# Layer norm 1 of a fused convolution-attention network: who issues the value weights, and where the turned tiles stand

## The chip, the core and the metric

The kernel runs on one core of a Trainium2 chip. The metric is the device time in microseconds (us); of several runs the median is given. Everything is in 32-bit floats.

The core's engines are TensorE (PE, with its weight loads as PEld), VectorE (DVE), ScalarE (ACT) and GpSimd (POOL). SyncE (SP) issues DMAs. Each engine works through its own instructions in order. DMAs are issued on SP's queue (q1 in the profile) or on GpSimd's (q0), and both feed the same 16 DMA engines.

## What is computed

The input is a feature map of 4 x 16 x 16 positions with 1024 channels, taken as 1024 tokens. Three layers follow one another, each added to its input:

```python
x = x + L0_conv(_gn(x))                    # group norm, then a position-dependent mixing ("lambda") layer
t = _to_tokens(x)                          # (4, 256, 1024)
t = t + L1_attn(_ln_t(t))                  # layer norm 1, causal attention with 16 heads
t = t + L1_ffn(_ln_t(t))                   # layer norm 2, eight experts behind a gate

def _ln_t(v, eps=1e-5):
    m = jnp.mean(v, axis=-1, keepdims=True)
    s = jnp.var(v, axis=-1, keepdims=True)
    return (v - m) / jnp.sqrt(s + eps)
# in L1_attn:
qkv = jnp.einsum('btc,oc->bto', x, W_attn) + b_attn     # q, k and v of every token
```

The change lies where the first layer's output becomes the attention's input: layer norm 1, and the first products for v.

## The kernel before

The 1024 tokens are eight tiles of 128 rows. A tile's rows lie on partitions, as the norm needs them; TensorE wants channels on partitions, so every normalised tile has to be transposed into `ln1`.

**One pass of the loop (lines 622 to 641).** `spread(i)` is the last part of the first layer. For the tile after the present one, `content` (L452) makes two products per bank, which VectorE adds to `s0` (L460). Then 16 products (L603) give the present tile's output, which VectorE adds to `xs[t]` (L610). `layer_norm` takes mean and variance on VectorE (L197, L199, `inverse_root` L141 to L143, L169), and ScalarE writes the normalised rows to one of three slices of the tile `ln_rows` (L170). GpSimd then adds the attention's output bias to `xs[t]` (L638) and stores it to DRAM as `x_rows` (L639). Tiles are taken in the order 1, 3, 5, 7, 0, 2, 4, 6 of the token tiles; "tile i" below is the i-th in that order.

**Two ways to transpose.** For tiles 0 to 5, `turn_by_rows` stores the normalised rows to DRAM on SP (L212), waits for that to land, and reads them back with four DMAs (`quarters_of`, L182), so that the 32-row groups stand where they belong. `turn_quarters` then transposes 32 x 32 blocks on VectorE (L187). The quarters' buffers are spare space: the tile `emb` for even tiles and `s_w` for odd ones among tiles 0 to 3, and two buffers of their own for tiles 4 and 5. The turn of tile i - 2 stands behind the norm of tile i. Tiles 6 and 7 are transposed on TensorE (L219) and copied out by ScalarE (L223).

**The order.** From line 621 to line 755 a manual schedule holds: every engine executes in the order in which the code issues. The value weights come as two halves of 2 MB each, `w_v0` and `w_v1`, loaded by `w_tile` (L129). `w_v0` is issued on SP in the fourth pass (i = 3), behind that tile's quarters. `w_v1` is issued on SP after the loop, and takes the memory of `ln_rows`.

**Behind the loop (lines 718 to 733).** GpSimd makes sums of blocks of `w_v0` (`sums_v`, L160 to L163), since v is computed by a scheme of seven block products instead of eight. `first(0, t)` makes products 1 and 2 for token tile t (two groups of eight, L665); ScalarE copies the first one's bank (L683) and `second` adds the other one on VectorE (L688). Token tiles 1 and 3 (tiles 0 and 1 of the loop) come first. Then follow the norm of tile 7, the transposes of tile 6, the turn of tile 5, the products for token tile 0, the transposes of tile 7, and the products for token tile 2. After that VectorE sums blocks of `ln1` (`sums_of_B`, L695 to L699) for the remaining products.

PSUM banks come from rings of three, `mm` and `tr`; a product waits until the bank's last reader is done.

Of the kernel before, what the change touches and what calls it, by code (L numbers as in the profile page):

```python
# [32 lines left out]
F32 = mybir.dt.float32  # L33
# [6 lines left out]
P = 128  # L40
C = 1024
# [4 lines left out]
NT = TOK // P  # L46
# [3 lines left out]
REL = 2 * SIDE - 1  # L50
# [7 lines left out]
HALF = 512  # L58
# [4 lines left out]
Q = 4  # L63
# [6 lines left out]
def kernel(  # L70
# [27 lines left out]
    nc = tc.nc  # L98

    def pool(stack, name, bufs=1, **kw):  # L100
        return stack.enter_context(tc.tile_pool(name=name, bufs=bufs, reuse_waits="tile", **kw))
# [21 lines left out]
    def w_tile(name, *parts, home=None, queue=nc.sync):  # L123

        w = (home or wpool).tile([P, NC, HALF], F32, tag="w", name=name)
        at = 0
        for part in parts:
            n = part.shape[1]
            queue.dma_start(w[:, :, at : at + n], part.rearrange("(c p) n -> p c n", p=P))  # L129
            at += n  # L130
        return w
# [7 lines left out]
    def inverse_root(dst, var, eps):  # L139

        nc.vector.tensor_scalar(dst, var, eps, None, ALU.add)  # L141
        nc.scalar.activation(dst, dst, AF.Sqrt)
        nc.vector.reciprocal(dst, dst)  # L143
# [23 lines left out]
    def normalised(row, of, mean, rstd):  # L167
        less = small.tile([P, 1], F32, tag="ln_less", name="ln_less")
        done = nc.vector.scalar_tensor_tensor(less, mean, -1.0, rstd, ALU.mult, ALU.mult)  # L169
        nc.scalar.activation(  # L170
            row.rearrange("p (f c i) -> p c f i", f=Q, c=NC),
            of.rearrange("p (c f i) -> p c f i", c=NC, f=Q),
            AF.Identity,
            bias=less,
            scale=rstd,
        )
        return done
# [7 lines left out]
    def turn(row_T, row, slots=P):  # L185

        nc.vector.transpose(  # L187
            row_T[:, :, :slots].rearrange("p c (g j) -> p g c j", j=32),
            row[:, : slots // 32, :].rearrange("p g (c i) -> p g c i", c=NC),
        )  # L190

    def layer_norm(ln, t, on_pe=False):


        stats = small.tile([P, 2, 6], F32, tag="ln_stats", name=f"ln1_stats{t}")
        for j in range(2):
            nc.vector.bn_stats(stats[:, j, :], xs[t][:, ts(j, HALF)])  # L197
        mv = small.tile([P, 2], F32, tag="ln_mv", name=f"ln1_mv{t}")
        nc.vector.bn_aggr(mv, stats)  # L199
        rstd = small.tile([P, 1], F32, tag="ln_rstd", name=f"ln1_rstd{t}")  # L200
        inverse_root(rstd, mv[:, 1:2], EPS)
        if on_pe:
            less = small.tile([P, 1], F32, tag="ln_less", name=f"ln1_less{t}")
            nc.vector.scalar_tensor_tensor(less, mv[:, 0:1], -1.0, rstd, ALU.mult, ALU.mult)
            for j in range(2):
                nc.scalar.activation(ln[:, ts(j, HALF)], xs[t][:, ts(j, HALF)], AF.Identity, bias=less, scale=rstd)
            return
        normalised(ln, xs[t], mv[:, 0:1], rstd)

    def turn_by_rows(ln, t, quarters, turns):  # L210
        rows = turns.tile([P, Q, C // Q], F32, tag="rows", name=f"ln1_rows{t}")
        nc.sync.dma_start(rows.rearrange("n f c -> n (f c)"), ln)  # L212
        quarters_of(rows, quarters)
# [7 lines left out]
    def turned_on_pe(dst, t, banks):  # L221
        for j, pt in enumerate(banks):
            nc.scalar.copy(dst[:, 4 * j : 4 * j + 4, ts(t, P)], pt.rearrange("p (c n) -> p c n", c=4))  # L223
# [3 lines left out]
    with ExitStack() as layer0:  # L227
        l0 = pool(layer0, "l0")
# [7 lines left out]
        vp = l0.tile([P, 4, 2], F32, tag="vp", name="vp")  # L236
        for i, a in enumerate((v_gamma, v_beta, v_mean, v_var)):
            nc.gpsimd.dma_start(vp[:, i, :], a)
        emb = l0.tile([P, 2, REL, REL], F32, tag="emb", name="emb")
        v_T = l0.tile([P, 2, TOK], F32, tag="v_T", name="v_T")  # L240

        q0 = l0.tile([P, 2, SIDE, SIDE, BH], F32, tag="q0", name="q0")
# [1 line left out]
        with ExitStack() as projection:  # L244
# [96 lines left out]
            with tc.manual_schedule():  # L341
# [6 lines left out]
                for c in range(NC):  # L348
# [10 lines left out]
                    elif NC - 4 < c < NC - 1:  # L359
                        n = c - (NC - 3)  # L360
# [15 lines left out]
            for pair in range(2):  # L376
                a = [xn[:, 4 * j : 4 * j + 4, ts(4 + 2 * pair + i, P)] for i in range(2) for j in range(2)]
# [9 lines left out]
            for n in (1, 2, 3, 5, 4, 7, 6):  # L387
                for pair, ((a11, a12, a21, a22), (c11, c12, c21, c22), (s1, s2, s3, s4)) in enumerate(pairs):
                    a, b = {
                        1: (a11, b11),  # L390
                        2: (a12, b21),
                        3: (s4, b22),
                        5: (s1, b11),
                        4: (a22, b21),
                        7: (s3, b12),
                        6: (s2, b22),
                    }[n]
# [133 lines left out]
        s_w = tpool.tile([P, 3, NC // 2, P], F32, tag="s_w", name="s_w", bufs=1)  # L531
# [46 lines left out]
        for b, nt in tiles:  # L578
            t = 2 * b + nt
# [6 lines left out]
        ln_rows = wpool.tile([P, 4, C], F32, tag="w", name="ln_rows")  # L586
# [4 lines left out]
        def spread(i):  # L591
            b, nt = tiles[i]
            t = 2 * b + nt
            if i == 0:
                content(b, nt)
            if i + 1 < NT:
                content(*tiles[i + 1])
            for hp in range(2):
                py = mm(f"py{t}_{hp}")
                for hl in range(2):  # L600
                    bh = b * HEADS0 + 2 * hp + hl
                    for mh in range(2):
                        nc.tensor.matmul(  # L603
                            py[:, ts(hl, M)],
                            s0[:, mh, ts(nt, S2), :, bh].rearrange("p i j -> p (i j)"),
                            v_T[:, mh, ts(b, M)],
                            start=(mh == 0),
                            stop=(mh == 1),
                        )
                nc.vector.tensor_add(xs[t][:, ts(hp, HALF)], xs[t][:, ts(hp, HALF)], py)  # L610
            return t

        def turn_quarters(i):
            of, quarters = to_turn[i]
            turn(ln1[:, :, ts(of, P)], quarters)

        spare = [
            of[:, :C].rearrange("p (f c) -> p f c", f=Q)
            for of in (emb.rearrange("p c i j -> p (c i j)"), s_w.rearrange("p a c n -> p (a c n)"))
        ]  # L620
        in_order.enter_context(tc.manual_schedule())
        for i in range(NT - 1):
            t = spread(i)
            quarters = None
            if i < NT - 2:
                if i < NT - 4:
                    quarters = spare[i % 2]
                else:
                    quarters = late.tile([P, Q, C // Q], F32, tag="xg", name=f"ln1_quarters{t}")
            to_turn.append((t, quarters))  # L630
            layer_norm(ln_rows[:, i % 3, :], t, i >= NT - 2)
            if i >= 2:
                turn_quarters(i - 2)
            if i < NT - 2:
                turn_by_rows(ln_rows[:, i % 3, :], t, quarters, turns)
                if i == 3:
                    w_v = [w_tile("w_v0", W_attnT[:, 2 * C : 2 * C + HALF])]
                nc.gpsimd.tensor_add(xs[t], xs[t], bp)  # L638
                nc.gpsimd.dma_start(x_rows[ts(t, P), :], xs[t])  # L639
            else:  # L640
                nc.sync.dma_start(x_rows[ts(t, P), :], xs[t])
        t = spread(NT - 1)
# [4 lines left out]
    with ExitStack() as attention:  # L647
# [31 lines left out]
        def homes(r, t):  # L679
            return [v1[2 * r + i][:, 4 * l + t, :] for i in range(2) for l in range(2)]  # L680

        def first(r, t, *tags):
            nc.scalar.copy(homes(r, t)[3], one(r, t, 1, *tags[:1]))  # L683
            return r, t, one(r, t, 2, *tags[1:])

        def second(r, t, bank):
            c11, c12, c21, c22 = homes(r, t)
            nc.vector.tensor_add(c11, bank, c22)  # L688
# [23 lines left out]
        def sums_v(r, engine):  # L712
            a11, a12, a21, a22 = blocks_v(r)
            s1, s2, s4 = (s_v[:, r, i, :, :] for i in range(3))
            sums_of_A(a11, a12, a21, a22, s1, s2, s4, engine)


        sums_v(0, nc.gpsimd)
        seconds = [first(0, 1, tr, tr), first(0, 3, mm, tr)]
        layer_norm(ln_rows[:, (NT - 1) % 3, :], t, True)  # L720
        two = ps.tile([P, 2, HALF], F32, tag="sc", name="ln_two", bufs=1)
        banks = two[:, 0, :], two[:, 1, :]
        turn_on_pe(ln_rows[:, (NT - 2) % 3, :], banks)
        turned_on_pe(ln1, to_turn[NT - 2][0], banks)
        turn_quarters(NT - 3)
        for done in seconds:
            second(*done)
        second(*first(0, 0, mm, mm))
        banks = tr("ln_pt0"), mm("ln_pt1")
        turn_on_pe(ln_rows[:, (NT - 1) % 3, :], banks)  # L730
        turned_on_pe(ln1, t, banks)
        second(*first(0, 2, tr, tr))
        x_home.close()
        sums = ExitStack()
# [196 lines left out]
        queue = [(pair, n) for pair in range(1, NPAIR - 2) for n in (1, 2, 6, 7, 4, 5, 3)]  # L931
# [166 lines left out]
    with ExitStack() as gating:  # L1098
# [6 lines left out]
        quarters = l2.tile([P, E], F32, tag="quarters", name="quarters")  # L1105
# [665 lines left out]
```

## Time and profile before

| what | us |
|---|---|
| median of 3 runs | 1221.26 (1220.8 to 1224.78) |
| the profiled execution: its own time | 1225.42 |
| the profiled execution: its span | 1223.6 |
| TensorE busy in the span | 1208.8 |
| VectorE busy | 719.4 |
| GpSimd busy | 404.7 |
| ScalarE busy | 203.9 |
| mean granted clock of TensorE, as a share of full speed | 0.998 |

Times in the timelines are counted from the start of the span; layer norm 1 lies between about 218 and 285 us. "Idle before" is the time an engine stood still ahead of an instruction, with the instruction or DMA that ended the wait. A granted clock of 1.00 is full speed.

### The profile page before, as it was taken

Reading aid. Unit: us, or ns where it says so; the run is one execution under the profiler, and the core shown is the slowest. Engines: PE = TensorE matmul, PEld = TensorE weight load, DVE = VectorE, ACT = ScalarE, POOL = GpSimd, SP = SyncE. Lnnn points to the kernel's source line nnn. Section 1 sums busy time; section 2 is a strip of 40 time slices with the busy share of each in tenths; the row PEclk is TensorE's granted clock in tenths of the full one; section 3 lists DMA queues with packets and bytes.
Section 4 is the critical chain, followed back from the end, with each engine's and each line's share of the span. In section 5 each row is a group of like instructions: output and inputs, shape, how many; then the busy total and the mean of one; then the engine's idle time right before and its main releaser. Section 6 shows DMA issues by size and latency. Waiting matters only on the chain.

```text
span 1223.6 us, 13265 instructions
## 1 busy us (share of the span) xinstructions
PE 1208.8 (99%) x4780; PEld 632.7 (52%) x4780; DVE 719.4 (59%) x1256; ACT 203.9 (17%) x505; POOL 404.7 (33%) x467
## 2 busy tenths in 40 slices
PE   9999999999999999999999999999999999999998
PEld 5444884777884444454544444444344334434443
DVE  5796636567423665566654657576565656565732
ACT  3310111111000222222221212101111111111110
POOL 1051341264000222222232117427453635463521
PEclk9999999999999999999999999999999999999999
DMA  9102014763202253525566746564855576556442
GB/s 349 27 1 69 18 42 116 257 233 112 69 1 69 91 172 106 166 89 169 159 199 191 245 173 234 158 175 95 244 160 142 113 226 189 138 141 179 96 83 54
DMA packets 94120, 169.77 MB, mean 139 GB/s; under 512 B 11968, under 2 KB 48848, under 8 KB 94048
## 3 DMA queue, kind: packets, MB, share of 16 engines
q1 hardware_dynamic: 73600, 108.49, 26.8%
q0 software_dynamic: 16144, 51.45, 17.7%
q10 hardware_dynamic: 4304, 8.91, 2.1%
q8 instruction: 40, 0.66, 0.2%
q14 instruction: 32, 0.26, 0.1%
HBM read 116.12 MB, written 48.50 MB: 135 GB/s over the span
## 4 chain that ended last, share of the span: by engine, by line
PE 90%; DMA 5%; DVE 2%; SPq 2%; issue 1%; ACT 0%; POOL 0%; DVEq 0%; POOLq 0%; ACTq 0%
PE p L1533 31%; PE pqk L665 15%; PE po L920 8%; PE pv L665 7%; PE pq_pair L400 4%; PE left L1575 3%; PE pq L319 3%; PE pT L510 3%; DMA ln_rows<-ln_rows 2%; PE pk L431 2%; PE sc L824 2%; PE pa L893 2%; PE rest L1589 2%; PE pv L538 2%; DMA s<-two_T 1%; PE last_pe L1696 1%
## 5 line engine op out<-in xcount | busy, mean ns | idle before, releaser
L1041 POOL DMA_INDIRECT w_e_xg<-rows,gather x146 | 156.5, 1072 | 51.9 <-issue 41.1
L1533 PE MATMUL p<-w_e,A 128*128 128x512 f32 x368 | 163.2, 593 | 0.0
L865 POOL TENSOR_TENSOR s_q<-s_q,total 128x128 f32<-128x128 f32 (+1 forms) x128 | 61.1, 513 | 277.1 <-DVE total L862 277.1
L1064 POOL DMA_INDIRECT out_dram<-y,add x32 | 57.3, 1790 | 175.7 <-ACT y L1539 113.5
L1533 PEld LDWEIGHTS p<-w_e,A 128*128 128x128 f32 x368 | 69.6, 190 | 88.5 <-issue 88.1
L920 PE MATMUL po<-w_p,y_T 128*128 128x512 f32 x256 | 114.9, 599 | 0.0
L1533 PE MATMUL p<-T,S 128*128 128x512 f32 x256 | 112.7, 593 | 0.0
L1539 ACT ACTIVATE y<-y,slot 128x512 f32<-128x512 f32 x64 | 46.0, 721 | 331.4 <-DVE y L1547 178.8
L665 PE MATMUL pqk<-ln,w_qk 128*128 128x512 f32 x192 | 85.7, 595 | 0.0
L1533 PEld LDWEIGHTS p<-T,S 128*128 128x128 f32 x256 | 48.6, 190 | 60.8 <-issue 60.5
L850 ACT ACTIVATE s_q<-sc,top 128x128 f32<-128x128 f32 (+1 forms) x128 | 52.1, 420 | 164.6 <-DVE top L846 121.2
L920 PEld LDWEIGHTS po<-w_p,y_T 128*128 128x128 f32 x256 | 47.1, 190 | 53.8 <-issue 52.8
L187 DVE STREAM_TRANSPOSE A<-w_e_xg 128x1024 f32<-128x1024 f32 x32 | 39.6, 1239 | 52.2 <-DMA w_e_xg<-rows,gather 52.2
L665 PEld LDWEIGHTS pqk<-ln,w_qk 128*128 128x128 f32 x192 | 36.1, 190 | 43.7 <-issue 42.1
L665 PE MATMUL pqk<-T,S_qk 128*128 128x512 f32 x128 | 57.8, 595 | 0.0
L1533 PE MATMUL p<-w_e,S 128*128 128x512 f32 x128 | 57.5, 592 | 0.0
L1533 PE MATMUL p<-T,A 128*128 128x512 f32 x128 | 57.5, 592 | 0.0
L665 PE MATMUL pv<-w_v,ln 128*128 128x256 f32 x192 | 45.4, 391 | 2.1 <-ACT ln L223 1.1
L319 PE MATMUL pq<-w_q,xn 128*128 128x512 f32 x96 | 44.5, 599 | 0.3 <-ACT xn L299 0.3
L1575 PE MATMUL left<-w_e,one 128*32 128x512 f32 x312 | 41.8, 593 | 0.0
L665 PEld LDWEIGHTS pv<-w_v,ln 128*128 128x128 f32 x192 | 37.4, 197 | 8.4 <-ACT ln L223 1.3
L880 DVE STREAM_TRANSPOSE s_T<-s_rows 128x768 f32<-128x768 f32 x32 | 30.3, 964 | 17.8 <-DMA s_rows<-s_rows 17.8
(333 smaller groups left out, 1828.4 us busy)
## 6 DMA issues: line engine op xcount, KB each, us to landing
w_e<-in_expert_w_dram SPq DMA_DIRECT2D x12, 2048.0 KB, 14.4
s_rows<-s_q SPq DMA_DIRECT2D x32, 384.0 KB, 2.3
s_rows<-s_rows SPq DMA_DIRECT2D x128, 96.0 KB, 2.4
w_qk<-in_W_attnT_dram SPq DMA_DIRECT2D x8, 1024.0 KB, 5.6
w_e<-in_expert_w_dram ACTq DMA_DIRECT2D x4, 2048.0 KB
xn<-in_xT_dram SPq DMA_DIRECT2D x8, 512.0 KB, 7.2
w_q<-in_Wq_dram SPq DMA_DIRECT2D x16, 256.0 KB, 6.6
x_at<-in_x_dram POOLq DMA_DIRECT2D x8, 512.0 KB
```

The lines of the kernel that those rows point to most:

```text
L187: nc.vector.transpose(row_T[:, :, :slots].rearrange("p c (g j) -> p g c j", j=32), row[:, : slots // 32, :].rearrange("p g (c i) -> p g c ...
L319: nc.tensor.matmul(pq, xn[:, c, ts(t, P)], w_q[kc][:, c, :], start=(c == 0), stop=(c == NC - 1))
L400: nc.tensor.matmul(bank, a[:, c, :], b[:, c, :], start=(c == 0), stop=(c == NC // 2 - 1))
L665: nc.tensor.matmul(bank, stationary(c), moving(c), start=(c == 0), stop=(c == NC // 2 - 1))
L850: nc.scalar.activation(blocks(h, qt), psc[:, h, cols].rearrange("p (b f i) -> p b f i", f=Q, i=32), AF.Exp, bias=top[:, qt, h : h + 1], sc ...
L865: nc.gpsimd.tensor_mul(blocks(h, qt), blocks(h, qt), total[:, qt, h : h + 1].unsqueeze(2).unsqueeze(3).to_broadcast([P, 1 + qt, Q, 32]),)
L920: nc.tensor.matmul(po, y_T[:, c, ts(t, P)], w_p[j][:, c, :], start=(c == 0), stop=(c == NC - 1))
L1041: nc.gpsimd.indirect_dma_start(out=row[:, g, :], out_offset=None, in_=table[: (TOK - P) * Q, :] if e in SHORT else table, in_offset=bass.I ...
L1064: nc.gpsimd.indirect_dma_start(out=out[: TOK - P, :] if e in SHORT else out, out_offset=bass.IndirectOffsetOnAxis(ap=add[:slots, e, k : k ...
L1533: nc.tensor.matmul(bank, a[:, c, :], b[:, c, :], start=(c == 0), stop=(c == NC // 2 - 1))
L1539: nc.scalar.mul(y[i][:, ts(j, HALF)], y[i][:, ts(j, HALF)], slot[:, e, 1, 2 * pair + i : 2 * pair + i + 1])
L1575: nc.tensor.matmul(bank[ts(i, 32), :], stationary, w[of][j][:, c, :], start=(c == 0), stop=(c == NC - 1))
```

## The change

The value weights' first half is issued by GpSimd in the third pass, after that tile's bias add and ahead of its store, instead of by SP in the fourth. Turns stand three tiles behind their norm instead of two. For that a third spare buffer is made: `emb` grows from 2 x 31 x 31 floats per partition to 2048, and its two halves and `s_w` take turns. Behind the loop, the norm of tile 7 is issued ahead of the products for token tiles 1 and 3, the turn of tile 4 (which used to be in the loop) stands behind tile 6's transposes, the turn of tile 5 behind the two `second` adds, and the transposes of tile 7 stand ahead of the products for token tile 0 instead of behind them.

```diff
-        emb = l0.tile([P, 2, REL, REL], F32, tag="emb", name="emb")
+        emb_at = l0.tile([P, 2 * C], F32, tag="emb", name="emb")
+        emb = emb_at[:, : 2 * REL * REL].rearrange("p (c i j) -> p c i j", c=2, i=REL)
...
         spare = [
-            of[:, :C].rearrange("p (f c) -> p f c", f=Q)
-            for of in (emb.rearrange("p c i j -> p (c i j)"), s_w.rearrange("p a c n -> p (a c n)"))
+            of.rearrange("p (f c) -> p f c", f=Q)
+            for of in (emb_at[:, :C], s_w.rearrange("p a c n -> p (a c n)")[:, :C], emb_at[:, C:])
         ]
...
                 if i < NT - 4:
-                    quarters = spare[i % 2]
+                    quarters = spare[i % 3]
...
             layer_norm(ln_rows[:, i % 3, :], t, i >= NT - 2)
-            if i >= 2:
-                turn_quarters(i - 2)
+            if i >= 3:
+                turn_quarters(i - 3)
             if i < NT - 2:
                 turn_by_rows(ln_rows[:, i % 3, :], t, quarters, turns)
-                if i == 3:
-                    w_v = [w_tile("w_v0", W_attnT[:, 2 * C : 2 * C + HALF])]
                 nc.gpsimd.tensor_add(xs[t], xs[t], bp)
+                if i == 2:
+                    w_v = [w_tile("w_v0", W_attnT[:, 2 * C : 2 * C + HALF], queue=nc.gpsimd)]
                 nc.gpsimd.dma_start(x_rows[ts(t, P), :], xs[t])
...
         sums_v(0, nc.gpsimd)
+        layer_norm(ln_rows[:, (NT - 1) % 3, :], t, True)
         seconds = [first(0, 1, tr, tr), first(0, 3, mm, tr)]
-        layer_norm(ln_rows[:, (NT - 1) % 3, :], t, True)
...
         turned_on_pe(ln1, to_turn[NT - 2][0], banks)
-        turn_quarters(NT - 3)
+        turn_quarters(NT - 4)
         for done in seconds:
             second(*done)
-        second(*first(0, 0, mm, mm))
+        turn_quarters(NT - 3)
         banks = tr("ln_pt0"), mm("ln_pt1")
         turn_on_pe(ln_rows[:, (NT - 1) % 3, :], banks)
         turned_on_pe(ln1, t, banks)
+        second(*first(0, 0, mm, mm))
         second(*first(0, 2, tr, tr))
```

## The prediction

> **What bounds the kernel now.** I read the page first. TensorE is busy 99% of the span, so only its idle or slowed time can be won.
>
> ```profile
> span 1223.6 us, 13265 instructions
> PE 1208.8 (99%) x4780; PEld 632.7 (52%) x4780; DVE 719.4 (59%) x1256; ACT 203.9 (17%) x505; POOL 404.7 (33%) x467
> ```
>
> Next I read TensorE's own timeline across layer norm 1 (238 to 286 us). The columns are start, length, operation and, in brackets, the idle time before it and what ended it.
>
> ```profile
> 239.68 3.70 PE L452 MATMUL pc<-q,k_q 128*128 128x512 f32 x8 [1.35 <-DVE s L460]
> ...
> 265.05 7.17 PE L665 MATMUL pv<-w_v,ln 128*128 128x256 f32 x32 [0.62 <-DMA w_v<-in_W_attnT_dram]
> 272.06 1.04 PE L219 MATMUL ln_two<-ident,ln_rows 128*128 128x128 f32 x8
> 273.46 3.69 PE L665 MATMUL pv<-w_v,ln 128*128 128x256 f32 x16 [0.36 <-DVE ln L187]
> 277.69 1.36 PE L219 MATMUL ln_pt<-ident,ln_rows 128*128 128x128 f32 x8 [0.54 <-ACT ln_rows L206]
> 280.11 5.41 PE L665 MATMUL pv<-w_v,ln 128*128 128x256 f32 x16 [1.06 <-ACT ln L223]
> ```
>
> Idle: 1.35 + 0.62 + 0.36 + 0.54 + 1.06 = 3.93. The second group of transposes takes 1.36 against 1.04 for the first, 0.32 more, because it waits for the second half of its row. The last group takes 5.41 where the same 16 products took 3.69, 1.72 more. The stretches show that the granted clock (the third number from the end) did that:
>
> ```profile
> 281.00:282.00 1.00, 1.00 (x4) 0.73 (x4) 0.00 (x0) 0.00 (x0) 0.00 (x0) 0.50 0.87 293
> ```
>
> Together 5.97 us. The causes are in the timelines of VectorE and of the SP queue, and in the chain of waits:
>
> ```profile
> 237.81 1.25 DVE L187 STREAM_TRANSPOSE ln<-emb 128x1024 f32<-128x1024 f32 x1 [3.48 <-DMA ln_rows<-ln_rows]
> ...
> 272.07 1.25 DVE L187 STREAM_TRANSPOSE ln<-ln_quarters 128x1024 f32<-128x1024 f32 x1 [8.22 <-DMA ln_quarters<-ln_rows]
> ```
> ```profile
> 247.51 3.56 DMA ln_rows<-ln_rows
> ...
> 253.09 0.40 SPq L129 DMA_DIRECT2D w_v<-in_W_attnT_dram x1
> ...
> 253.59 13.65 DMA ln_rows<-ln_rows
> ```
>
> VectorE runs in order. The turn of row tile 0 holds it 3.48 us, and the bank evictions behind it hold TensorE 1.35. Row tile 4's store follows the 2 MB w_v0 in SP's queue and takes 13.65 us where tile 3's took 3.56. So tile 4's turn holds VectorE 8.22 us, and tile 7's adds, its norm, the norm's ScalarE pass and TensorE's transposes all queue behind that turn.
>
> **The change part by part.** Tile numbers follow the order of the loop.
>
> *Turns three behind.* Turn 0 now follows norm 3, which VectorE reaches at about 241.3 (norm 3 takes 2.1 us and starts some 2.1 earlier than its 241.34, without the held adds). Its data were there by 237.81. The 1.35 goes, and everything behind moves 1.35 earlier; tile 7's spread ends at 264.43 - 1.35 = 263.08. VectorE still does six turns at 1.25.
>
> *The third spare* issues nothing. Tile 2 goes into the second half of the emb tile instead of where tile 0 lay.
>
> *w_v0 on GpSimd.* SP loses 0.40 us of issue; GpSimd gains one issue. x_at's rows took 0.53 each, and bv, which like w_v0 comes in 1024 pieces, 0.92; I take 0.9. It runs after tile 2's add, at about 238.1, and delays x_rows 2 and the later adds behind it. GpSimd idled 3.3 to 6.2 us ahead of each add, so this costs nothing. The load spent 11.9 us from issue to landing at its old place; even 14 us puts it at 253, ten before TensorE wants it. The 0.62 goes.
>
> Here a rule speaks against the change. The Trainium skill, "DMA: Bandwidth & Descriptors", section "Rules for kernel authors", says that spreading DMAs over SP, ACT and GpSimd gives no bandwidth, only sequencer time. By that rule moving the load is worth its 0.40 us of issue. By the rows it is worth more, because here order counts, not bandwidth: 13.65 - 3.56 = 10.1 us of SP's chain is one small store queued behind one large load. I take the row.
>
> The price on the other side: two queues now share the engines. While x_at loaded (213 to 217 us), GpSimd's queue moved 1.22 MB and SP's 0.19 MB:
>
> ```profile
> q0 software_dynamic: 333, 1.22, 87.1%
> q1 hardware_dynamic: 254, 0.19, 16.1%
> ```
>
> At that rate w_v0's 2.1 MB last 2.1 / 0.305 = 6.9 us. SP's chain, which undisturbed moves about 0.17 MB per us, moves 0.05, so it loses 6.9 x 0.12 / 0.17 = 5 us. That is the upper end. The packet counts there are similar (333 and 254), so with w_v0's 2 KB pieces against quarters of 1 KB and rows of 4 KB I expect 2 to 3 us. It is covered. Undisturbed, stores come 5.6 to 7 us apart: rows 4 at 253, rows 5 at 259, its quarters in at about 267. With 3 to 5 us more that is 270 to 272, and TensorE needs turn 5 done by 275.8 (below), so its data by 274.5. Turn 1 has the least time: its data came at 244.5 before, 247 to 249.5 now, and VectorE comes to it at 248.4. TensorE only feels a wait if it lasts beyond 250.7, when the next bank would be late. Cost 0, ends 0 and 1.
>
> *The last norm ahead of older turns.* From 263.08 TensorE does 32 products (7.07, to 270.15), 16 transposes (2.1, to 272.25), then products 0 and 2 (6.9, to 279.15). VectorE: turn 3 from 262.5, adds of tile 7 to 265.0, its norm to 267.5; ScalarE writes the row by 269.1. The last transposes want it at 271.2, so the 0.54 and 0.32 are covered by 2 us. What queues behind this norm on ScalarE are the two L683 copies. They now run at 269.1 to 269.8, and TensorE needs their bank at 271.2. Turn 4 follows at 267.5 and is needed at 272.25, so the 0.36 goes. ScalarE's bank copies (1.05 for two) then run beside products 0, which need neither, so the 1.06 goes.
>
> *The clock.* With no gap there is no reason for 3.41 us at half speed: 1.71 less. A second rule warns. The Trainium skill, "TensorE: Matmul & The Clock Gate", section "Part 4: PE-mode transpose", says that a transpose does not count as busy the way a matmul does. The two groups now stand back to back, 2.1 us out of a stretch as long as the slow one (3.41). By the rule that may look idle and keep the loss of 1.71. By the rows: the drop followed a stretch of 3.41 us whose share of matmuls was 0.13 and of transposes 0.38, by the starts and ends in the trace; shares of 0.68 and 0.30 (269.9 to 273.3) brought none. The new stretch has a share of at least 0.38 of matmuls and no gap, between these; nearer the second in total work. I take no drop.
>
> *A stall that moves.* The sums on VectorE just behind this stage lie close to TensorE:
>
> ```profile
> 286.11 1.22 DVE L695 TENSOR_TENSOR T<-ln 128x1024 f32<-128x1024 f32 x1
> 287.37 3.38 DVE L696 TENSOR_TENSOR T<-ln,T 128x1024 f32<-128x1024 f32 x1
> 290.68 3.37 DVE L698 TENSOR_TENSOR ln<-ln 128x1024 f32<-128x1024 f32 x1
> ```
>
> They take 3.37 instead of 1.22 while GpSimd sums w_v1 (from 287.32). The third ends at 294.05, and the product that reads it starts at 294.19: no slack. w_v1 is issued when the last transposes free its slot and reaches GpSimd 8.27 us after they end (279.05 to 287.32). The first sum came 7.06 after them, and now comes 6.9 + 0.59 = 7.49 after them, since both products lie between. So GpSimd starts 0.78 after it, not 1.21. The 0.43 left of that sum takes 0.43 x 2.76 = 1.2, about 0.8 more, and TensorE waits 0.7. Ends: 0, if w_v1 lands half a microsecond later, and 2.0, if it lands before the sums.
>
> Sum: 5.97 - 0.7 = 5.2 us, a profiled span of 1218.4 and its own time 1225.4 - 5.2 = 1220.2. That execution stood 4.2 above the median of the runs, so part of its loss (the clock, most easily) may be missing there. Taking all 5.2 off the median gives 1216.1.
>
> **The rivals.**
> - *The clock is worth nothing*: it drops in the new stretch too, or did not in the median run. Gain 5.2 - 1.7 = 3.5, 1217.8. For it: the back-to-back transposes and the 4.2 us. Against it: no gap is left.
> - *SP's chain starves* as rows 4 did, by 10 us. Turn 1 gets its data at 254.5, and TensorE waits 3.8, once, since later turns shift with it: 5.2 - 3.8 = 1.4, 1219.9. For it: the 0.19 MB. Against it: that row stood in one queue with the load.
> - *Slower: the two halves of emb count as one tile.* Then turn 0 waits for tile 2's quarters, which land at about 252.5, not 237.8. VectorE stops from 241.3; TensorE's next bank, due at 245.5, comes at 252.5 + 1.25 + 0.6 = 254.3: 8.8 us idle, and 1.7 for the clock behind so long a gap. -5.2 + 10.5 = +5.3, 1226.6. It decides from turn 0 starting after about 250.7. Against it: ScalarE began writing ln_rows' second slice at 227.43, while the store that reads the first was only issued at 227.69. Slices are told apart there.
>
> **How the numbers follow.** Forecast 0.60, clock 0.18, starved chain 0.11, one tile 0.08; 0.03 for anything else. The range runs from all 5.97 and one more us (1214.3) to just past the starved chain (1220.4). Within 0.3% (3.7 us, about what a measurement of this kernel can tell from no change) means above 1217.6: the forecast mostly lies below it, the clock case on the line. Faster 0.66, same 0.22, slower 0.12.
>
> **What would show it.** No idle ahead of L452 near 239; rows 4 issued to landed under 6 us; w_v0 in before 256; turns 4 and 5 with no wait that TensorE feels; both groups of transposes together in about 2.1 us; clock 1.00 throughout; a wait of 0 to 2 us on L698 before the seventh product. A turn 0 held past 250, or a second store over 10 us, would prove me wrong.

## The result and the profile after

The changed kernel takes 1219.97 us (median of 19 runs, 1217.08 to 1222.44); the kernel before, run beside it, 1223.87. The ratio is 0.9970 (95% interval 0.9961 to 0.9979), a gain of 0.30% or 3.7 us where 5.2 us (0.42%) were forecast. Two later comparisons of the same two kernels gave 0.9978 (0.9965 to 0.9991) and 0.9981 (0.9972 to 0.9990): about half the forecast.

In absolute time 1219.97 lies 3.9 us above the forecast 1216.1, but 2.6 of these are not the change's: the kernel before itself took 1223.87 in this comparison, not the 1221.26 from which the forecast was taken.

The two profiled executions differ by twice the measured gain: 1225.42 before, 1217.96 after. The page of the changed kernel:

```profile
span 1216.2 us, 13286 instructions
PE 1205.4 (99%) x4780; PEld 631.6 (52%) x4780; DVE 718.7 (59%) x1256; ACT 203.9 (17%) x505; POOL 405.1 (33%) x468
...
PE 96%; DVE 2%; DMA 1%; issue 0%; SPq 0%; ACT 0%; POOL 0%; DVEq 0%; POOLq 0%; ACTq 0%
```

The last line is the chain that ended last: TensorE holds 96% of it in this execution and DMA 1%, where before it was 90% and 5%. That difference is one of executions more than of kernels: in the two later profiles of the changed kernel TensorE holds 88% and 93%. TensorE's timeline across layer norm 1 (lines have moved: L603 is now L604, L665 L666):

```profile
237.64 3.60 PE L453 MATMUL pc<-q,k_q 128*128 128x512 f32 x8
241.07 3.67 PE L604 MATMUL py<-v_T,s 128*128 128x256 f32 x16
...
255.00 7.25 PE L604 MATMUL py<-v_T,s 128*128 128x256 f32 x32
262.08 7.07 PE L666 MATMUL pv<-w_v,ln 128*128 128x256 f32 x32
268.99 1.04 PE L219 MATMUL ln_two<-ident,ln_rows 128*128 128x128 f32 x8
269.87 1.04 PE L219 MATMUL ln_pt<-ident,ln_rows 128*128 128x128 f32 x8
270.74 7.07 PE L666 MATMUL pv<-w_v,ln 128*128 128x256 f32 x32
277.65 7.07 PE L666 MATMUL pv<-s_v,ln 128*128 128x256 f32 x32
```

No line has an idle time in brackets: all five waits are gone in this execution, as forecast. SP's queue and VectorE tell how. Columns are start and length. A store's time, here and below, runs from its issue to the issue of the quarters behind it, which wait for its landing; time that it spends behind earlier transfers in SP's queue is in it.

```profile
238.67 0.39 SPq L212 DMA_DIRECT2D ln_rows<-ln_rows  x1
248.70 2.36 SPq L182 DMA_DIRECT2D emb<-ln_rows  x4
...
257.39 0.38 SPq L212 DMA_DIRECT2D ln_rows<-ln_rows  x1
260.93 1.86 SPq L182 DMA_DIRECT2D ln_quarters<-ln_rows  x4
```
```profile
240.80 1.25 DVE L187 STREAM_TRANSPOSE ln<-emb 128x1024 f32<-128x1024 f32 x1
247.74 1.25 DVE L187 STREAM_TRANSPOSE ln<-s_w 128x1024 f32<-128x1024 f32 x1
```

Tile 4's store takes 3.5 us, but tile 2's now takes 10.0. The starved store has moved. In this execution the lag of three keeps the turns from feeling it.

### The profile page after: what moved, and what is told of

It is laid out like the page before. It is cut to its first block, busy times and chain, and to the rows that moved or that the text cites. A ratio compares the mean times of both kernels' runs of the same rounds, so it can differ in the third digit from the quotient of the medians.

```text
span 1216.2 us, 13286 instructions
## 1 busy us (share of the span) xinstructions
PE 1205.4 (99%) x4780; PEld 631.6 (52%) x4780; DVE 718.7 (59%) x1256; ACT 203.9 (17%) x505; POOL 405.1 (33%) x468
## 4 chain that ended last, share of the span: by engine, by line
PE 96%; DVE 2%; DMA 1%; issue 0%; SPq 0%; ACT 0%; POOL 0%; DVEq 0%; POOLq 0%; ACTq 0%
PE p L1535 32%; PE pqk L666 15%; PE po L922 8%; PE pv L666 8%; PE pq_pair L401 4%; PE left L1577 3%; PE pq L320 3%; PE pT L511 3%; PE py L604 2%; PE pk L432 2%; PE pc L453 2%; PE pv L539 2%; PE sc L826 2%; PE pa L895 2%; PE rest L1591 2%; PE last_pe L1698 1%
## 5 line engine op out<-in xcount | busy, mean ns | idle before, releaser
L666 PE MATMUL pqk<-ln,w_qk 128*128 128x512 f32 x192 | 85.7, 595 | 0.0
L666 PEld LDWEIGHTS pqk<-ln,w_qk 128*128 128x128 f32 x192 | 36.1, 190 | 43.7 <-issue 42.1
L666 PE MATMUL pqk<-T,S_qk 128*128 128x512 f32 x128 | 57.8, 595 | 0.0
L666 PE MATMUL pv<-w_v,ln 128*128 128x256 f32 x192 | 43.2, 379 | 0.0
L1535 PEld LDWEIGHTS p<-w_e,S 128*128 128x128 f32 x128 | 24.3, 190 | 30.6 <-issue 30.1
L1535 PEld LDWEIGHTS p<-T,A 128*128 128x128 f32 x128 | 24.3, 190 | 30.6 <-issue 30.4
```

What stands on the lines that cost most here:

```text
L666: nc.tensor.matmul(bank, stationary(c), moving(c), start=(c == 0), stop=(c == NC // 2 - 1))
L1535: nc.tensor.matmul(bank, a[:, c, :], b[:, c, :], start=(c == 0), stop=(c == NC // 2 - 1))
```

## The experiments

One measure is used throughout. The *stage* runs from the start of tile 2's spread products (the third group; two expectations call it the fourth) to the start of the first product that reads the sums (`pv<-s_v,ln`). In the changed kernel's first profile it is 277.65 - 227.13 = 50.52 us; with no idle time in it, that is its floor. Ratios are to the kernel before on the same chip.

### The kernel before again, three more profiles

No edit.

> The kernel before, once more, for a second profile and for the spread of its runs. The first profile stood 1.6 us above the median of 19 runs and lost 7.2 us in layer norm 1 (238 to 286 us) that the changed kernel did not. Theory 1: that execution was a bad one, and a typical execution loses only 3 to 5 us there (smaller gaps, or no 3.41 us at half clock). Theory 2: the stage loses its 7 us in every execution, and the changed kernel loses about 3 us somewhere else in a typical execution. Timed against itself: 1.000, within 0.001.

> A third profile of the kernel before, to see whether layer norm 1 loses about 1 us, as in the second, or 7, as in the first. If the losses depend on how soon tile 0's store lands (5.05 us in the first, 3.02 in the second): one of 3 us goes with a loss near 1 us, one of 5 us with 4 us or more.

> The kernel before, a fourth profile, and its times against itself on the same chip: 1.000 within 0.001. The stage from the fourth group of spread products to the first product with sums took 57.7, 51.8 and 53.3 us in three profiles of before: 51 to 54 us if the first was the odd one.

Against itself: 1.0002 (0.9991 to 1.0013) and 1.0004 (0.9993 to 1.0015); the third is a single run without a comparison. The stages are 57.67 (the first profile), 51.79, 53.34 and 53.38 us. So it is theory 1, as far as four profiles tell: none of the others comes near the execution that I had read. They lose 1.3 to 2.9 us against the floor, not 7.2. Two things limit this. The three ran 0.9 to 1.4 us faster than the medians beside them (1220.77 against 1221.69, 1219.65 against 1221.02, 1220.03 against 1220.93), so a typical execution may lose more. And of the 19 runs of before beside the change, three were slower still than the profiled 1225.42. TensorE's timeline in the fourth profile:

```profile
237.77 3.70 PE L452 MATMUL pc<-q,k_q 128*128 128x512 f32 x8
...
262.41 7.17 PE L665 MATMUL pv<-w_v,ln 128*128 128x256 f32 x32
...
274.48 1.36 PE L219 MATMUL ln_pt<-ident,ln_rows 128*128 128x128 f32 x8 [0.54 <-ACT ln_rows L206]
276.90 3.72 PE L665 MATMUL pv<-w_v,ln 128*128 128x256 f32 x16 [1.06 <-ACT ln L223]
```

The waits of 0.54 and 1.06 around the last transposes are there again, but not the 1.35 ahead of L452 nor the 0.62 for w_v0. And the 16 products after them take 3.72, not 5.41: behind the same two waits the clock stays at 1.00.

```profile
277.00:281.00 4.00, 4.00 (x19) 3.54 (x20) 0.28 (x1) 0.71 (x2) 0.00 (x0) 1.00 0.91 305
```

Tile 0's store landed in 3.0, 3.0 and 3.5 us in these three, 5.0 in the first. That goes with the turn that held TensorE 1.35 us there, and not here. Two experiments below that keep the lag of two fit it: with stores of 5.0 (`only_queue`) and 4.7 us (`only_tail`) TensorE stood 1.38 and 1.16 us at this place. The time of the store doesn't set the whole loss, though: the second of the three (`b_third`) has a store of 3.0 and loses 2.8, not the 1 that I expected, in waits of 0.33, 0.38 and 1.06 further on.

### The queue alone

```diff
-                if i == 3:
-                    w_v = [w_tile("w_v0", W_attnT[:, 2 * C : 2 * C + HALF])]
                 nc.gpsimd.tensor_add(xs[t], xs[t], bp)
+                if i == 2:
+                    w_v = [w_tile("w_v0", W_attnT[:, 2 * C : 2 * C + HALF], queue=nc.gpsimd)]
```

> Before, with w_v0 issued by GpSimd in the third pass and nothing else. If the load in SP's queue is the main cause (my prediction's reading): row tile 4's store takes under 6 us, turns 4 and 5 no longer hold VectorE, so 0.62, 0.36 and most of 0.54, 1.06 and the clock's 1.7 go: a gain of 3 to 4 us; the 1.35 at turn 0 stays and may grow. If the rule on spreading DMAs is right: no more than 0.4 us.

Measured: 1.0033 (1.0020 to 1.0046), slower, and a stage of 60.15 us. The part that I had thought the core of the gain costs 4 us by itself. Its SP queue, VectorE, TensorE and clock:

```profile
237.27 1.81 SPq L182 DMA_DIRECT2D s_w<-ln_rows  x4
239.18 0.50 SPq L212 DMA_DIRECT2D ln_rows<-ln_rows  x1
250.16 1.89 SPq L182 DMA_DIRECT2D emb<-ln_rows  x4
```
```profile
249.06 1.25 DVE L187 STREAM_TRANSPOSE ln<-s_w 128x1024 f32<-128x1024 f32 x1 [6.72 <-DMA s_w<-ln_rows]
```
```profile
250.94 5.55 PE L452 MATMUL pc<-q,k_q 128*128 128x512 f32 x8 [5.33 <-DVE s L460]
```
```profile
251.00:254.00 3.00, 3.00 (x4) 1.45 (x5) 2.97 (x6) 0.00 (x0) 0.00 (x0) 0.50 0.77 227
```

Tile 4's store does get fast (3.5), but GpSimd issues w_v0 at 236.6, and everything on SP beside it is slow: tile 1's quarters (`s_w`), the last of them issued at 238.57 and landed 10.37 us later, and tile 2's store behind them, 11.0 us. Turn 1 waits for those quarters. Without the lag it holds VectorE 6.7 us, TensorE stands 5.33, and the clock is halved for 6.83 us, from 247.88 on. It is what the rival of the starved chain described, in the kernel without the lag. Neither expectation foresaw a loss; that the move gains no more than 0.4 us did come true.

### Everything but the queue

```diff
                 turn_by_rows(ln_rows[:, i % 3, :], t, quarters, turns)
+                if i == 3:
+                    w_v = [w_tile("w_v0", W_attnT[:, 2 * C : 2 * C + HALF])]
                 nc.gpsimd.tensor_add(xs[t], xs[t], bp)
-                if i == 2:
-                    w_v = [w_tile("w_v0", W_attnT[:, 2 * C : 2 * C + HALF], queue=nc.gpsimd)]
```

> The changed kernel, but w_v0 on SP in the fourth pass, as before. Theory of the queue: tile 4's store takes over 10 us again, the quarters of tiles 4 and 5 come late; the new order in the tail lets TensorE do products for token tiles 1 and 3 and both transposes first, so it waits for turn 4 only at about 271 (data at 272): a wait of 1 to 3 us, and a time 2 to 4 us above the changed kernel. Rival (lag and tail order are what counts): within 1 us of the changed kernel.

> The changed kernel with w_v0 on SP in the fourth pass, a second time. If the queue part is worth nothing beside lag and tail order: a ratio to before of 0.997 to 0.999, as for the changed kernel (0.9970, 0.9978, 0.9981). If it carries a part of the gain: 0.9985 or above, as far as intervals tell. Tile 4's store takes 10 to 13 us, and TensorE's stage is 51 to 53 us.

Measured: 0.9982 (0.9974 to 0.9990) and 0.9987 (0.9975 to 0.9998); stages 51.19 and 53.26. That is a gain of about 2 us without the queue part. In the first of them tile 4's store takes 11.5 us, yet TensorE waits only 0.40 for it in the whole stage, because lag and tail leave it other work:

```profile
270.00 1.04 PE L219 MATMUL ln_pt<-ident,ln_rows 128*128 128x128 f32 x8
270.88 3.62 PE L666 MATMUL pv<-w_v,ln 128*128 128x256 f32 x16
274.89 3.72 PE L666 MATMUL pv<-w_v,ln 128*128 128x256 f32 x16 [0.40 <-DVE ln L187]
```

For this profile my expectation of 1 to 3 us was too high. The second one has a wait of 1.21 for w_v0 and one of 1.00 here. The ratio 0.9987 lies in both of the ranges that I had set for the second run, so it doesn't decide between them. Against the whole change (0.9970, 0.9978, 0.9981) the intervals overlap: the means, 0.9976 and 0.9985, differ by 0.0008, about as much as the noise allows. What the queue adds to the other two, if anything, isn't settled.

### The old order in the tail, and each part alone

`old_tail` is the changed kernel with the old order behind the loop; `only_lag` has w_v0 on SP as well; `only_tail` is the kernel before with the new tail. The edit of the first:

```diff
-        layer_norm(ln_rows[:, (NT - 1) % 3, :], t, True)
         seconds = [first(0, 1, tr, tr), first(0, 3, mm, tr)]
+        layer_norm(ln_rows[:, (NT - 1) % 3, :], t, True)
...
         turn_quarters(NT - 3)
+        second(*first(0, 0, mm, mm))
         banks = tr("ln_pt0"), mm("ln_pt1")
         turn_on_pe(ln_rows[:, (NT - 1) % 3, :], banks)
         turned_on_pe(ln1, t, banks)
-        second(*first(0, 0, mm, mm))
```

> The changed kernel with the old order behind the loop: tile 7's norm behind the first products, its transposes behind the products for token tile 0. If the order in the tail counts: ScalarE's copies of the last transposes come right ahead of the products of token tile 2, so about 1.1 us of idle time comes back, with 1.7 for the clock if that drops: 1 to 3 us above the changed kernel. If only queue and lag count: within 0.5 us of it.

> Before, with turns three behind and the third spare, but w_v0 on SP and the old order in the tail. If the lag is a full share of the gain: the idle time at L452 (1.35 us in one profile of before, none in the other) never appears, and VectorE's adds of tile 7 no longer stand behind turn 4; ScalarE's copies ahead of token tile 2's products still cost about 1 us. Ratio 0.998 to 0.9995. If the lag needs the tail order: 1.000.

> Before, with the tail reordered (tile 4's turn behind tile 6's transposes, tile 7's norm first, both groups of transposes together), lag two and w_v0 on SP. If the hold of tile 7's adds behind turn 4 was the main loss: the 1.06 and the clock go, turn 0's wait may stay: ratio 0.998 to 0.999. If the lag is what counts: above 0.9995.

| version | ratio to before | stage, us |
|---|---|---|
| queue and lag (old tail) | 0.9988 (0.9978 to 0.9997) | 52.53 |
| lag alone | 0.9998 (0.9985 to 1.0010) | 52.50 |
| tail alone | 0.9987 (0.9977 to 0.9997) | 54.53 |

The lag alone gives nothing that can be measured; the tail alone gives 0.13%. Both together gave 0.18 and 0.13%. So the tail's order is the part that can be seen to pay by itself, and its ratio is in the range expected if the hold of tile 7's adds behind turn 4 was the main loss. The profiles don't show it more closely. The 1.06 is gone with the new tail, but that execution (1221.15, the slowest of its 11) has waits of 1.16, 0.78 and 1.29 elsewhere, and its stage of 54.53 is longer than three of before's four. And with the old tail the 1.1 us ahead of token tile 2's products did not come back as expected: the waits there are 0.41 and 0.86 at other places.

### The changed kernel again, twice

No edit.

> The changed kernel once more, beside the partial ones on one chip. Theory now: lag and tail order carry the gain, and the queue adds nothing or little, because w_v0 on GpSimd's queue starves tile 2's store (10.0 us in its first profile) instead of tile 4's, and the lag covers it. So a ratio to before of 0.997 to 0.9985, within 0.001 of the version without the queue part (0.9982). Rival (the load's place in SP's queue is what counts): at least 0.0015 better than that version. Layer norm 1 again without idle time on TensorE.

> The changed kernel a third time, beside the two improvements. Ratio to before 0.997 to 0.998, as in the first two; its stage between 50.5 us (first profile) and 53.6 (second), by whether tile 2's store takes 10 us or 12.

The stages are 53.64 and 52.70, against 50.52 in the first profile. So the changed kernel's first profile was a good draw, as the other's was a bad one. Tile 1's quarters and tile 2's store behind them are slower here (the store takes 12.0 and 12.8 us), and then the lag no longer covers them. VectorE and TensorE in the third profile:

```profile
250.61 1.25 DVE L187 STREAM_TRANSPOSE ln<-s_w 128x1024 f32<-128x1024 f32 x1 [3.02 <-DMA s_w<-ln_rows]
```
```profile
252.48 3.70 PE L453 MATMUL pc<-q,k_q 128*128 128x512 f32 x8 [0.89 <-DVE s L461]
```

Turn 1 waits for tile 1's quarters and starts at 250.61, and TensorE's next bank comes 0.89 us late. In the second profile the wait stood elsewhere: 0.92 at the last spread products, behind turn 2, for which tile 2's store came too late, and 1.47 ahead of the last transposes.

The stages of single profiles don't account for the gain. With 53.64 and 52.70 the changed kernel's are no shorter than the 51.79 to 53.38 of before, while the medians beside them differ by 2.3 and 2.6 us. The executions are not typical ones: these two ran 1.2 and 1.8 us slower than their medians (1218.74 and 1217.02), the three of before 0.9 to 1.4 faster, and outside the stage the four profiles of before alone differ by 2.6 us. That the gain lies in this stage is what the change and the waits argue; no profile of a median execution shows it.

### A product with one tensor operand

That 1.47 went back to one small instruction of VectorE, the 128x1 product behind the norm, in the second profile of the changed kernel. ScalarE's norm pass (L206) waits 2.56 us for it, and the copies behind that pass (L684) free the bank for TensorE. The second fence is GpSimd at the same time, the third ScalarE and TensorE.

```profile
268.40 0.16 DVE L143 RECIPROCAL ln_rstd<-ln_rstd 128x1 f32<-128x1 f32 x1 [0.27 <-ACT ln_rstd L142]
268.60 2.25 DVE L204 SCALAR_TENSOR_TENSOR ln_less<-ln_mv,ln_rstd 128x1 f32<-128x1 f32 x1
```
```profile
268.48 2.35 POOL L162 TENSOR_TENSOR s_v<-w_v,s_v 128x1024 f32<-128x1024 f32 x1
```
```profile
270.93 1.52 ACT L206 ACTIVATE ln_rows<-x_at,ln_less,ln_rstd 128x512 f32<-128x512 f32 x2 [2.56 <-DVE ln_less L204]
272.76 1.09 PE L219 MATMUL ln_pt<-ident,ln_rows 128*128 128x128 f32 x8 [1.47 <-ACT v L684]
```

It takes 2.25 us instead of 0.16 and ends when GpSimd's sum does. (The L141 of the same norm, with one tensor operand, took 0.15 from 267.98, in the middle of the sum before, which ran from 266.05 to 268.41.) The experiment gives the second factor as a per-partition scalar:

```diff
-            nc.vector.scalar_tensor_tensor(less, mv[:, 0:1], -1.0, rstd, ALU.mult, ALU.mult)
+            nc.vector.tensor_scalar(less, mv[:, 0:1], rstd, -1.0, ALU.mult, ALU.mult)
```

> The changed kernel; the 128x1 product behind tile 6's and tile 7's norm (L204) takes its second factor as a per-partition scalar instead of a second tensor. In the changed kernel that instruction took 0.96 and 2.25 us instead of 0.16 and ended when GpSimd's sum ended, and in the second profile TensorE waited 1.47 us for it. If two tensor operands in SBUF are what makes VectorE wait for GpSimd: 0.16 us beside GpSimd's sums, no wait of TensorE at the last transposes, and 0 to 1 us less in the median. If any small instruction waits beside GpSimd: 0.9 to 2.3 us again.

```profile
267.36 0.21 DVE L204 TENSOR_SCALAR ln_less<-ln_mv,ln_rstd 128x1 f32<-128x1 f32 x1
```
```profile
264.98 2.35 POOL L161 TENSOR_TENSOR s_v<-s_v,w_v 128x1024 f32<-128x1024 f32 x1
267.40 2.37 POOL L162 TENSOR_TENSOR s_v<-w_v,s_v 128x1024 f32<-128x1024 f32 x1
```

It takes 0.21 us and TensorE has no wait at the last transposes. But it happened to run across the seam between two sums (one ends at 267.33, the next begins at 267.40), so this profile doesn't show how it would do in the middle of one. In the time no gain shows: 0.9989 (0.9980 to 0.9998) beside the changed kernel's 0.9981, a median 0.97 us higher where 0 to 1 us lower was expected; the intervals overlap. The wait is gone where it stood, and another (0.75 ahead of the last products) bounds the stage at 52.29.

### The load in four parts on SP

```diff
+                if i == 1:
+                    w_v = [wpool.tile([P, NC, HALF], F32, tag="w", name="w_v0")]
+                if 1 <= i <= 4:
+                    some = slice(2 * (i - 1), 2 * i)
+                    nc.sync.dma_start(
+                        w_v[0][:, some, :],
+                        W_attnT[ts(i - 1, 2 * P), 2 * C : 2 * C + HALF].rearrange("(c p) n -> p c n", p=P),
+                    )
                 nc.gpsimd.tensor_add(xs[t], xs[t], bp)
-                if i == 2:
-                    w_v = [w_tile("w_v0", W_attnT[:, 2 * C : 2 * C + HALF], queue=nc.gpsimd)]
```

`split_one` has the one-operand product too; `split_early` puts the parts into passes 0 to 3.

> The changed kernel, but w_v0 on SP in four parts of 512 KB, one behind the quarters of each of the tiles 1 to 4. If a store starves because one large load stands beside or ahead of it: no store takes over 7 us (10.0 and 12.0 in the changed kernel for tile 2), turns 1 to 3 never hold VectorE long enough for TensorE to feel it, and the median is 0 to 1.5 us below the changed kernel's. If the bytes are what counts, whatever the order: the chain ends as late, turns 4 and 5 hold TensorE 1 to 3 us.

> Both: w_v0 in four parts on SP and the one-operand product. If both waits are real and separate, layer norm 1 has no idle time on TensorE at all, at 50.5 us from the fourth group of spread products to the first product with sums, and the median is 1 to 2 us below the changed kernel's: ratio to before 0.996 to 0.9975. If the parts come too late for the turns of tiles 4 and 5: no better than the changed kernel.

> The changed kernel with w_v0 in four parts of 512 KB on SP behind the quarters of tiles 0 to 3. Behind tiles 1 to 4 the last part was issued at 266.5 us, after TensorE wanted it, and cost 6.8 us and the clock. Behind tiles 0 to 3 it is issued at about 258 and in by 261, before TensorE's 262: if the late part was the whole loss, no wait for w_v0, and a ratio of 0.996 to 0.998. If four stores of 6 us push the turns of tiles 4 and 5 back: TensorE waits 2 to 5 us at product 0 or 2, and it is no better than before.

Measured: 1.0047 (1.0033 to 1.0060), 1.0059 (1.0045 to 1.0072) and 1.0003 (0.9994 to 1.0013). In the first, no store took over 6.3 us, as expected, and turns 0 to 3 never waited. But every part was issued only behind a store's landing and the quarters, and the last one at 266.5, after TensorE wanted it:

```profile
272.16 7.11 PE L672 MATMUL pv<-w_v,ln 128*128 128x256 f32 x20 [6.81 <-DMA w_v<-in_W_attnT_dram]
```

With earlier parts TensorE still waits 1.76 us for the last one, 1.55 and 1.54 later on; its stage is 56.09. The four stores with a part ahead of them take 6.0 to 6.8 us and make the chain late. So the bytes count as well as the order; the expected gain did not come, and none of these versions beats the changed kernel.

## Why the prediction was wrong in size, step by step

- **The sum: this step failed.** "Taking all 5.2 off the median" put the losses of one execution on all of them. Of the terms, only the 1.06 is in all four profiles of before (0.97 to 1.06). The 1.35, the 0.36 and the 1.71 for the clock are in one; the 0.62 is in one, with 0.33 in another; the 0.54 is in two, with 0.38 in a third. That one execution's stage lost 7.2 us, even more than 5.97, since a break of TensorE's row costs some overlap too (from 234.62 to 243.22 us the break of 1.35 cost 1.61). The other three lost 1.3 to 2.9, and the changed kernel's own lose 0 to 3.1. I had seen the execution stand 4.2 us above the median of three runs and made it a remark. Against the 19 runs beside the change it stood 1.55 above (1223.87), and 5.2 - 1.55 = 3.65 is about what was measured there; that is arithmetic, not a cause shown.
- **Turn 0 and the 1.35 us.** The mechanism is right: in no profile of the changed kernel does turn 0 wait. But before loses the 1.35 only where tile 0's store takes 5 us, in one of four profiles.
- **w_v0 on GpSimd: SP's chain "2 to 3 us" later, "cost 0, ends 0 and 1".** The delay was mis-sized. Tile 2's store took 10.0 to 12.8 us, 5 to 8 more than the 4.5 to 5.2 of before. The rate of the x_at load that I had shown and then discounted was close to the true one. I had reckoned with w_v0 in 2 KB pieces; between 242 and 248 us of the second profile after, the queues moved

```profile
q0 software_dynamic: 417, 1.64, 80.8%
q1 hardware_dynamic: 406, 0.40, 21.9%
```

  which is 3.9 KB per packet on GpSimd's queue against 1.0 KB on SP's, and about as many packets on each. Packets of 1.0 KB are the quarters, a stored row being 4 KB: what crawled here was tile 1's quarters, and tile 2's store stood behind them. I had named turn 1 as the one with the least time, with data at 247 to 249.5; it started at 247.7 without a wait, and at 249.4 and 250.6 when its data came. So TensorE lost little to the delay, 0, 0.92 and 1.11 us (0.89 and 0.22) in the three profiles, up to just past my range; the lag hid the rest. The Trainium skill's rule that spreading DMAs over engines gains no bandwidth ("DMA: Bandwidth & Descriptors", "Rules for kernel authors"), which I had set aside, fits: w_v0 took 11.9 us before and 11.5 in the third profile after. It doesn't say that the move can cost, as it did alone (4 us).
- **The tail.** Right in order and within 2 us in time: transposes at 268.99 and 269.87 (I had 270.15 and 271.2, with a span that began 0.5 later), no wait in the first profile. What I left out is that tile 7's norm now runs beside GpSimd's sums: its small product took 0.96, 2.25 and 0.47 us, and cost TensorE 1.47 in one profile.
- **The clock.** No drop behind 16 transposes in a row, in the first and third profile of the changed kernel (in the second the 1.47 parted them, and there was no drop either): the rule on transposes (the Trainium skill, "TensorE: Matmul & The Clock Gate", "Part 4: PE-mode transpose") took nothing here. But the 1.71 to be won was in one of four profiles of before, and absent from another with the same two waits. That speaks for the rival "did not in the median run".
- **The stall that moves, 0.7 us.** It did not come. The first sum came 7.5 us behind the transposes, as worked out; GpSimd's start came 11.0 behind them (270.91 to 281.91), not 8.27, so the three first sums ran at 1.22 to 1.23.
- **The rivals.** The measured 1219.97 falls on the starved chain's 1219.9 by luck: its wait of 3.8 us came in no profile of the changed kernel. One tile is refuted: turn 0 started at 240.80, before tile 2's quarters were issued at 248.70, so the halves of emb are told apart.

What stays open: how often the bad stage of before comes up, with four profiles; how much of the median's gain lies in this stage; and what the queue part is worth in the whole.

## What to carry to other kernels

If a profiled execution stands well above the median, profile the kernel again before summing its waits: here four profiles of one stage gave losses of 1.3 to 7.2 us. A large load moved to another queue doesn't vanish; here it starved the small transfers beside it at its new place, so move one only under work that has slack for that. And each part of a combined change should be timed alone: the part that looked like the core was a loss without the others.

## What the runs showed of the hardware

- **VectorE waited for GpSimd a whole instruction at a time.** An instruction with two tensor operands in SBUF, even of 128x1, ended with GpSimd's running sum (0.16 became 0.47 to 2.25 us in the changed kernel). The 128x1024 sums of VectorE took 3.37 instead of 1.22 beside GpSimd's, and GpSimd's 3.21 instead of 2.36. One with a single tensor operand took its usual 0.15 in the middle of such a sum.
- **The same waits halved TensorE's clock in one execution and not in another; where they fell on a grid of 3.41 us fits the difference.** Within a trace, the times at which the granted clock changed differ by whole multiples of 3.41 us: in the first profile of before 280.15, 283.56 and, at the program's end, 1222.22 (1 and 276 steps). There the waits of 0.54 and 1.06 us lie in one cell of that grid, 276.73 to 280.15, in which TensorE was busy 1.78 of 3.42 us, and in the next cell the clock was 0.50. In the fourth profile the grid, counted back from the change at 1214.15, has an edge at 275.48 between the same two waits. TensorE was busy 2.82 and 2.36 us in the two cells, and the clock stayed at 1.00, as it did after a cell with 1.94 in the second profile of the changed kernel (269.39 to 272.80). At waits of 5.33 and 6.81 us the clock was 0.50 for 6.83 us, two cells. No run moved a wait along the grid on purpose, so this is a fit, not a test.
